# A graph network with sorted neighbours on one core: the gates of the gathers are moved from VectorE to ScalarE

## The chip, the cores and the metric

The kernel runs on one core of a Trainium2 chip. The metric is device time in microseconds (us). Engines are named as in the profile: PE (TensorE), DVE (VectorE), ACT (ScalarE), POOL (GpSimd) and SP (SyncE). Each works through its own list of instructions in order and waits for the others by semaphores. DMAs are issued by SP and, where rows are gathered by index, by POOL.

## The reference

There are 16 graphs of 1024 nodes with 64 channels, and four layers, each a layer norm and a residual around one step on the same adjacency matrix. Cut to what matters:

```python
h = relu(layernorm(x)); x = x + tanh(concat(h, adj @ h) @ W1 + b1) @ W2 + b2        # layer 0
h = relu(layernorm(x)); x = x + (adj + I) @ h / rowsum(adj + I)                     # layer 1
h = relu(layernorm(x)); x = x + mlp(h + quantiles(h of the kept neighbours)) * mask # layer 2
h = relu(layernorm(x)); x = x + (adj @ h) * inv_deg @ W_neighbors + h @ W_self + b  # layer 3
```

Layer 2 is the long one. In a node with more than ten neighbours it removes every k-th neighbour (on both sides of an edge), and then takes for each node and channel the 25%, 50% and 75% quantiles over the neighbours that are left, weighted 0.25, 0.5 and 0.25.

## The kernel before, in words

Each graph passes through six streams, which are Python generators: `adjacency` (load, transpose, find the neighbours to remove, order the nodes by their number of neighbours), `layers` (layers 0 and 1 and the norm of layer 2), `neighbour_lists` (the neighbours' numbers of each node, by repeated top-8 searches on DVE), `gathers`, `sorts` and `tail` (rest of layer 2, layer 3). Several graphs are under way at once.

The nodes are ordered by degree and cut into eight blocks of 128, in five groups k0 to k4 (`GROUPS`). For each group, `gathers` (L1239) fetches the feature rows of the neighbours with one indirect DMA on POOL for each place and block, 128 rows of 256 bytes (L1275): 124 gathers in a graph, 1984 in all, into a single-buffered tile `raw0` to `raw4`. `sorts` runs a pruned sorting network over that tile on DVE (L1308, between `raw` and `other`) and sums the wanted places with their weights (L1327). Places beyond a block's fill are filled by ACT (L1251). POOL also loads key rows for the lists (L1088), packed rows of the few longest nodes (L1256), and gathers the results back to node order (L1347).

The order of all instructions is made when the program is built. A planner (`Clock`, L812) keeps four clocks, `dve`, `pe`, `act` and `pool`. Every stream adds its costs to them by hand and yields the planned time at which it wants to go on; the loop at the end of `direct_path` always resumes the first stream in its list that is due at `clk.dve`, and sets `clk.dve` forward when none is due. `after` (L818) adds the costs of a step to the clocks. A gather adds 1.39 to `clk.pool`, and `gathers` yields `clk.pool - 5` after four of them. So the planner's clocks decide where each instruction stands in its engine's list; the chip decides when it runs.

The gate ties POOL to that plan. Before every four gathers, and before the first key loads of a graph, `gate` (L914) is called. If `clk.dve` is over 3.0 past the last mark, DVE writes a one-element memset (L917), the mark, at its present place in the list, and POOL copies that element (L919), so that it waits until DVE has come as far as the plan had it when these gathers were put in. Eight slots of the mark are used in turn.

Other lines that the text speaks of: preln on DVE and ACT (L848 to L858), where DVE's reduction L853 reads what ACT squared (L851) and L856 what ACT rooted (L854); the neighbour counts that ACT makes in `adjacency` (L956) and DVE adds (L964); signs and keys on ACT (L1024, L1027), positions (L1047, L1050); the eight activations that sum the rows of the transposed adjacency matrix in `layers` (L1212), behind which the planner adds ten units to `clk.act`; the division of layer 1 (L1219).

Of the kernel before, what the change touches and what calls it, by code (L numbers as in the profile page):

```python
# [7 lines left out]
F32 = mybir.dt.float32  # L8
F16 = mybir.dt.float16
BF = mybir.dt.bfloat16  # L10
I32 = mybir.dt.int32
# [6 lines left out]
P = 128  # L18
C = 64
NB = 8  # L20
# [711 lines left out]
def direct_path(ctx: ExitStack, tc: tile.TileContext, t: dict, out: bass.AP, flag):  # L732
# [3 lines left out]
    nc = tc.nc  # L736
# [3 lines left out]
    const = ctx.enter_context(tc.tile_pool(name="const", bufs=1))  # L740
    loads = ctx.enter_context(tc.tile_pool(name="loads", bufs=2))
    graph = ctx.enter_context(tc.tile_pool(name="graph", bufs=1))
    nodes = ctx.enter_context(tc.tile_pool(name="nodes", bufs=2))
# [19 lines left out]
    eps = const.tile([P, 1], F32, name="eps")  # L763
# [51 lines left out]

    clk = Clock()

    def after(dve=0.0, pe=0.0, act=0.0, lat=0.3):  # L818

        clk.dve += dve  # L820
        at = clk.dve
        if pe:
            clk.pe = at = max(clk.pe, at) + pe
        if act:
            clk.act = at = max(clk.act, at) + act
        return at + lat


# [14 lines left out]
    def preln(u, x, ha):  # L843

        s = nodes.tile([P, 4, NB], F32, name="stat")
        xc = mid(u, [P, NB, C])
        sq = mid(u, [P, NB, C])
        nc.vector.tensor_reduce(s[:, 0], x, AX.X, ALU.add)  # L848
        ts(s[:, 1], s[:, 0], 1.0 / C, None, op0=ALU.mult)
        tt(xc, x, s[:, 1, :, None].to_broadcast([P, NB, C]), ALU.subtract)  # L850
        act(sq, xc, AF.Square)  # L851
        yield after(1.5, act=0.65, lat=1.2)
        nc.vector.tensor_reduce(s[:, 2], sq, AX.X, ALU.add)  # L853
        act(s[:, 3], s[:, 2], AF.Sqrt, bias=eps, scale=1.0 / C)  # L854
        yield after(0.7, act=1.0, lat=1.5)
        nc.vector.reciprocal(s[:, 2], s[:, 3])  # L856
        tt(xc, xc, s[:, 2, :, None].to_broadcast([P, NB, C]), ALU.mult)
        act(ha[:, :, :C], xc, AF.Relu)  # L858
        yield after(0.9, act=0.65)
# [45 lines left out]
    def even(v, u):  # L905

        return v.rearrange("c (q u p) -> c u q p", u=2, p=P)[:, u]


    marks = []  # L910
    slots = const.tile([1, 8], F32, name="mark")
    opened = const.tile([1, 2], F32, name="gate")

    def gate():  # L914
        if not marks or clk.dve > marks[-1] + 3.0:
            k = len(marks)
            nc.vector.memset(slots[:, k % 8:k % 8 + 1], 0.0)  # L917
            clk.dve += 0.15
            nc.gpsimd.tensor_copy(opened[:, k % 2:k % 2 + 1], slots[:, k % 8:k % 8 + 1])  # L919
            marks.append(clk.dve)  # L920


    state = [dict() for _ in range(B)]
# [11 lines left out]
    def adjacency(b):  # L935
# [91 lines left out]
            act(p, p, AF.Sign, accum_out=ms[:, i:i + 1])  # L1027
            yield after(0, pe=4.5, act=2.3) - 4.0

        mv = nodes.tile([P, NB], F32, name="mv")  # L1030
        act(mv, ms, AF.Copy, bias=512.0, scale=0.5)
        yield clk.act + 2.0
        key = nodes.tile([P, NB], F32, name="key")
        nc.vector.scalar_tensor_tensor(key, ms, 512.0, cn8, op0=ALU.mult, op1=ALU.add)
        neg = nodes.tile([P, NB], F32, name="neg")
        ts(neg, key, -1.0, None, op0=ALU.mult)
        p = bank2()
        for q in range(2):
# [2 lines left out]
               key[:, 4 * q:4 * q + 4, None].to_broadcast([P, 4, P]), ALU.mult)  # L1041
            nc.tensor.matmul(p[:, q * 512:(q + 1) * 512], onesf, spread.rearrange("p j m -> p (j m)"),
                             start=True, stop=True)
        over = nodes.tile([P, NB], F32, name="over")
        for i in range(NB):
            sink = lists.tile([P, N], F16, tag="ab", name="sink")
            act(sink, p, AF.Sign, bias=neg[:, i:i + 1], accum_out=over[:, i:i + 1])  # L1047
# [1 line left out]
        pos = nodes.tile([P, NB], I32, name="pos", bufs=5)  # L1049
        ts(pos, over, 0.5, 511.5, op0=ALU.mult, op1=ALU.add)  # L1050

        pi = nodes.tile([P, 2, NB], I32, name="pi")
        ts(pi[:, 0], pos, P - 1, None, op0=ALU.bitwise_and)
        ts(pi[:, 1], pos, 7, None, op0=ALU.arith_shift_right)
        ph = nodes.tile([P, 2, NB], F16, name="ph")
        nc.vector.tensor_copy(ph, pi)
        low = lists.tile([P, NB, P], F16, tag="ab", name="low")
        tt(low, pidx[:, None, :].to_broadcast([P, NB, P]), ph[:, 0, :, None].to_broadcast([P, NB, P]), ALU.is_equal)
        high = nodes.tile([P, NB, NB], F16, name="high")
        tt(high, pidx[:, None, :NB].to_broadcast([P, NB, NB]), ph[:, 1, :, None].to_broadcast([P, NB, NB]),  # L1060
           ALU.is_equal)
        both = nodes.tile([P, 2, NB, NB], F16, name="both")
        tt(both[:, 0], high, nid[:, :, None].to_broadcast([P, NB, NB]), ALU.mult)
        tt(both[:, 1], high, mv[:, :, None].to_broadcast([P, NB, NB]), ALU.mult)
        p = bank()
# [3 lines left out]
        m = nodes.tile([P, NB], F32, name="m", bufs=3)  # L1069
# [9 lines left out]
    def neighbour_lists(b):  # L1079
# [5 lines left out]
        def load_keys(i):  # L1085
            if i < NB:
# [4 lines left out]
                ks.append((k, clk.pool + 3.5))  # L1091

        gate()
        for i in range(KB):
            load_keys(i)
# [143 lines left out]
    def gathers(b):  # L1239
        g = state[b]  # L1240
        yield max(g["rows_at"], clk.pool)
        for k, (b0, n, cap, *_) in enumerate(GROUPS):
# [17 lines left out]
            for s in range(cap):  # L1260
                if s % (4 // n) == 0:
                    gate()
                if k == 0 and s == 9:
                    for l, size in enumerate(sizes):
                        nc.sync.dma_start(rows_d[l, :size], packed[:size, l * C:(l + 1) * C])
                if k == 0 and s == 17:
                    for l, p0, s0, ns, nn in PACKS:
                        nc.sync.dma_start(raw[:nn, s0:s0 + ns, :],
                                          rows_d[l, p0:p0 + ns * nn].rearrange("(n s) c -> n s c", s=ns))
                for i in range(n):  # L1270
                    if s >= PLACES[b0 + i]:
                        continue
                    clk.pool += 1.39
                    at = sum(LISTS[:b0 + i]) + s
                    nc.gpsimd.indirect_dma_start(raw[:, s, i * C:(i + 1) * C], None, h_ds[b % 3],  # L1275
                                                 bass.IndirectOffsetOnAxis(ap=g["index"][:, at:at + 1], axis=0))
                if (s + 1) % (4 // n) == 0:
                    yield clk.pool - 5
# [142 lines left out]
    def over_graphs(step, *needs):  # L1421
# [5 lines left out]

    streams = [
        over_graphs(adjacency, ("adjt", 1), ("keys", 1), ("sorts", 3)),
        over_graphs(layers, ("rows", 0), ("tail", 3)),  # L1430
        over_graphs(tail, ("sorts", 0)),
# [23 lines left out]
                assert soonest is not None  # L1455
                clk.dve = soonest

    one = nodes.tile([P, 1], F32, name="one")
    nc.vector.tensor_reduce(one, bad, AX.X, ALU.max)
    p = bank()  # L1460
    nc.tensor.matmul(p[:1, :1], one, onesf[:, :1], start=True, stop=True)
# [3 lines left out]
@with_exitstack  # L1465
def kernel(ctx: ExitStack, tc: tile.TileContext, t: dict, out: bass.AP):
    nc = tc.nc
    pool = ctx.enter_context(tc.tile_pool(name="flag", bufs=1))
    flag = pool.tile([1, 1], I32, name="flag")
    direct_path(tc, t, out, flag)  # L1470
    many = nc.values_load(flag[:1, :1], min_val=0, max_val=P)
    with tc.If(many > 0):
        general_path(tc, t, out)
# [106 lines left out]
```

## Time and profile before

| | |
|---|---|
| median of three runs | 3909.36 us (3884.14 to 3925.28) |
| profiled execution | 3897.33 us, of which the span on the core is 3895.5 us |
| busy DVE / POOL / PE / ACT | 3035.7 / 2644.1 / 2044.1 / 1410.1 us |
| gathers L1275 | 1984, 2148.8 us busy, 1083 ns each in the mean |
| gate copies L919 on POOL | 477, 163.9 us busy, 344 ns each in the mean |
| ACT, one-column-of-eight operations | L1070 (copy from PSUM) 163 ns, L1031 205 ns |
| table loads on ACT | 34 in all, 1283 ns each |

How to read it: busy time is time in which an engine executes, without its waits. A line of a wait list says who waited, for whom, for how many us in total, how often and how long at most. A line of the stretches gives start and end, length, busy time of the five engines with their instruction counts, then the granted clock of PE as a share of full speed, the share of the DMA engines and GB/s. In the chain of waits the profile follows the work back from the last instruction.

### The profile page before, as it was taken

Reading aid. Unit: us, or ns where it says so; the run is one execution under the profiler, and the core shown is the slowest. Engines: PE = TensorE matmul, PEld = TensorE weight load, DVE = VectorE, ACT = ScalarE, POOL = GpSimd, SP = SyncE. Lnnn points to the kernel's source line nnn. Section 1 sums busy time; section 2 is a strip of 40 time slices with the busy share of each in tenths; the row PEclk is TensorE's granted clock in tenths of the full one; section 3 lists DMA queues with packets and bytes.
Section 4 is the critical chain, followed back from the end, with each engine's and each line's share of the span. In section 5 each row is a group of like instructions: output and inputs, shape, how many; then the busy total and the mean of one; then the engine's idle time right before and its main releaser. Section 6 shows DMA issues by size and latency. Waiting matters only on the chain.

```text
span 3895.5 us, 32579 instructions
## 1 busy us (share of the span) xinstructions
PE 2044.1 (52%) x8483; PEld 988.9 (25%) x8483; DVE 3035.7 (78%) x7309; ACT 1410.1 (36%) x2658; POOL 2644.1 (68%) x2792
## 2 busy tenths in 40 slices
PE   6464554646654574646446474565556555741113
PEld 3222222223222232222222232232222323220101
DVE  1557878879687897888787798899699876979482
ACT  5444334243433434333332443443344433430000
POOL 1077576776667686776776777777778686777781
PEclk8666667677676686676666777767677676765555
DMA  2313234152423425242341524243343423232121
GB/s 89 124 39 115 50 99 117 45 172 46 141 68 101 120 65 154 70 125 69 106 106 45 175 51 153 56 142 80 100 119 104 116 55 123 68 105 58 42 52 55
DMA packets 237348, 362.43 MB, mean 93 GB/s; under 512 B 126848, under 2 KB 128496, under 8 KB 237152
## 3 DMA queue, kind: packets, MB, share of 16 engines
q1 hardware_dynamic: 156912, 255.00, 19.0%
q0 software_dynamic: 80096, 104.70, 13.5%
q8 instruction: 69, 1.13, 0.1%
q14 instruction: 127, 1.04, 0.1%
q10 hardware_dynamic: 144, 0.56, 0.0%
HBM read 245.26 MB, written 114.81 MB: 92 GB/s over the span
## 4 chain that ended last, share of the span: by engine, by line
DVE 42%; issue 14%; PE 12%; another core or an unknown queue 9%; ACT 8%; POOL 8%; DMA 5%; SPq 0%; DVEq 0%; ACTq 0%; POOLq 0%
DVE other L1308 12%; DVE raw L1308 11%; POOL raw L1275 6%; PE pt L877 5%; DVE most L1117 4%; ACT adjt L1212 2%; DVE found L1103 2%; DVE agg L1327 2%; ACT sink L1047 2%; DMA k<-keys_d,node 1%; DMA raw<-h_d,index 1%; PE pt L901 1%; DVE k L1112 1%; DVE nb L942 1%
## 5 line engine op out<-in xcount | busy, mean ns | idle before, releaser
L1275 POOL DMA_INDIRECT raw<-h_d,index x1984 | 2148.8, 1083 | 559.0 <-issue 533.1
L1308 DVE TENSOR_TENSOR other<-raw 128x512 f32<-128x512 f32 (+11 forms) x816 | 536.7, 688 | 151.7 <-DMA raw<-h_d,index 113.9
L877 PE MATMUL pt<-adjt,ha 128*65 128x512 f32 (+1 forms) x1024 | 485.4, 635 | 44.6 <-DVE ha L1199 30.6
L919 POOL COPY gate<-mark 1x1 f32<-1x1 f32 x477 | 163.9, 344 | 416.2 <-DVE mark L917 369.3
L949 PE MATMUL pt<-ef,a 128*128 128x128 f32 x1024 | 207.5, 360 | 320.8 <-ACT adjt L950 129.6
L1308 DVE TENSOR_TENSOR raw<-other 128x512 f32<-128x512 f32 (+10 forms) x464 | 355.9, 792 | 5.8 <-DVE other L1308 0.6
L991 PE MATMUL pt<-eh,nbt 128*128 128x512 f16 (+3 forms) x1024 | 213.8, 365 | 266.5 <-ACT nbt L980 192.2
L1117 DVE MAX8 most<-k 128x8 uint16<-128x1024 uint16 x208 | 255.4, 1228 | 13.2 <-DVE k L1112 3.3
L949 PEld LDWEIGHTS pt<-ef,a 128*128 128x128 f32 x1024 | 157.7, 185 | 408.2 <-issue 180.6
L1024 ACT ACTIVATE nb<-pt 128x1024 f16<-128x1024 f32 x128 | 130.6, 1020 | 317.1 <-remote 118.4
L877 PEld LDWEIGHTS pt<-adjt,ha 128*65 128x65 f32 (+1 forms) x1024 | 148.1, 148 | 364.1 <-issue 360.1
L950 ACT COPY adjt<-pt 128x512 f32<-128x512 f32 x256 | 139.1, 583 | 250.0 <-remote 146.4
L956 ACT ACTIVATE nb<-nb 128x512 f16<-128x512 f16 x256 | 159.6, 629 | 179.3 <-DVE nb L942 70.2
L1308 DVE TENSOR_TENSOR raw<-other,raw 128x640 f32<-128x640 f32 (+3 forms) x448 | 216.5, 494 | 4.9
L1308 DVE TENSOR_TENSOR raw<-raw,other 128x128 f32<-128x128 f32 (+7 forms) x496 | 211.5, 436 | 6.1
L1020 PE MATMUL pt<-eh,gone 128*128 128x128 f16 x1024 | 129.7, 257 | 162.7 <-DVE gone L1000 76.5
L878 ACT COPY big<-pt 64x1024 f32<-64x1024 f32 (+1 forms) x32 | 32.2, 1007 | 496.1 <-PE pt L877 300.6
L1308 DVE TENSOR_TENSOR other<-other,raw 128x128 f32<-128x128 f32 (+4 forms) x448 | 201.4, 460 | 4.2
L1384 PE MATMUL tm<-at,ha 128*64 128x512 f32 x512 | 174.1, 785 | 50.0 <-DMA at<-adjt_d 44.4
L1103 DVE MAX8 found<-k 128x8 f32<-128x1024 f16 x128 | 156.3, 1221 | 51.2 <-DMA k<-keys_d,node 51.2
L991 PEld LDWEIGHTS <-nbt 128*128 128x128 f16 x1024 | 105.0, 116 | 359.4 <-ACT nbt L980 203.2
L1347 POOL DMA_INDIRECT res<-agg_d,pos x128 | 135.7, 1060 | 74.9 <-DMA agg_d<-agg 37.4
(182 smaller groups left out, 4350.6 us busy)
## 6 DMA issues: line engine op xcount, KB each, us to landing
a<-in_adj_dram SPq DMA_DIRECT2D x64, 1024.0 KB
adjt_d<-adjt SPq DMA_DIRECT2D x64, 1024.0 KB
at<-adjt_d SPq DMA_DIRECT2D x128, 512.0 KB
keys_d<-nb SPq DMA_DIRECT2D x64, 512.0 KB
raw<-h_d,index POOLq DMA_INDIRECT x1984
x<-in_x_dram SPq DMA_DIRECT2D x16, 256.0 KB
h_d<-h SPq DMA_DIRECT2D x16, 256.0 KB
agg_d<-agg SPq DMA_DIRECT2D x16, 256.0 KB
```

The costliest lines, as they stand in the source:

```text
L877: nc.tensor.matmul(p[p0:p0 + n, s], h[:, j, :n], adjt[:, j, s], start=j == 0, stop=j == NB - 1)
L919: nc.gpsimd.tensor_copy(opened[:, k % 2:k % 2 + 1], slots[:, k % 8:k % 8 + 1])
L949: nc.tensor.transpose(p[:, u * P:(u + 1) * P], a[:, j * P:(j + 1) * P], identf)
L950: nc.scalar.copy(adjt[:, 4 * q:4 * q + 4, i * P:(i + 1) * P], p.rearrange("p (u m) -> p u m", m=P))
L956: act(nb[:, i, s], nb[:, i, s], AF.Copy, accum_out=mn[:, q, i:i + 1])
L991: nc.tensor.matmul(p[:, o:e], nbt[:, j, :], stair[:, :e - o], start=j % 4 == 0, stop=j % 4 == 3)
L1103: nc.vector.max(out=found[:, o:o + 8], in_=src)
L1117: nc.vector.max(out=most, in_=less.bitcast(U16))
L1275: nc.gpsimd.indirect_dma_start(raw[:, s, i * C:(i + 1) * C], None, h_ds[b % 3], bass.IndirectOffsetOnAxis(ap=g["index"][:, at:at + 1], axi ...
L1308: tt(view(two[to], *((i, vi) if greater else (j, vj)), w), view(two[s], i, vi, w), view(two[u], j, vj, w), ALU.max if greater else ALU.min)
L1347: nc.gpsimd.indirect_dma_start(res[:, i, :], None, g["agg_d"], bass.IndirectOffsetOnAxis(ap=g["pos"][:, i:i + 1], axis=0))
L1384: nc.tensor.matmul(p[q * C:(q + 1) * C, :], ha[:, j, :], even(ats[j], q), start=j == 0, stop=j == NB - 1)
```

## The change

`gate` no longer makes a mark. A new function `mark`, called in `after` whenever a step has a cost on ACT, makes ACT copy one element into a slot behind the work just planned, if `clk.act` is over 3.0 past the last mark; it adds 0.2 to `clk.act`. Some steps that the planner charges to ACT by hand make no mark. `gate` looks through the last 20 marks for the latest whose planned time lies more than 1.0 before `clk.pool`, and lets POOL copy it; if there is none, or it is the one that was waited for last, it does nothing. There are 32 slots. In the built programs the 477 memsets on DVE and 477 copies on POOL become 513 copies on ACT and 363 copies on POOL. As marks no longer add 0.15 to `clk.dve` but 0.2 to `clk.act`, other instructions change their places too. The tiles `mv`, `key`, `neg`, `over`, `pi`, `ph`, `high`, `both` and `one` have one buffer in place of two.

```diff
+    marks, gates = [], []
+    slots = const.tile([1, 32], F32, name="mark")
+    opened = const.tile([1, 2], F32, name="gate")
+
+    def mark():
+        if not marks or clk.act > marks[-1][0] + 3.0:
+            t = slots[:, len(marks) % 32:len(marks) % 32 + 1]
+            nc.scalar.copy(t, eps[:1])
+            clk.act += 0.2
+            marks.append((clk.act, t))
+
+    def gate():
+
+        due = [m for m in marks[-20:] if m[0] < clk.pool - 1.0]
+        if due and gates[-1:] != due[-1:]:
+            gates.append(due[-1])
+            nc.gpsimd.tensor_copy(opened[:, len(gates) % 2:len(gates) % 2 + 1], due[-1][1])
+
     def after(dve=0.0, pe=0.0, act=0.0, lat=0.3):
...
         if act:
             clk.act = at = max(clk.act, at) + act
+            mark()
         return at + lat
...
-    marks = []
-    slots = const.tile([1, 8], F32, name="mark")
-    opened = const.tile([1, 2], F32, name="gate")
-
-    def gate():
-        if not marks or clk.dve > marks[-1] + 3.0:
-            k = len(marks)
-            nc.vector.memset(slots[:, k % 8:k % 8 + 1], 0.0)
-            clk.dve += 0.15
-            nc.gpsimd.tensor_copy(opened[:, k % 2:k % 2 + 1], slots[:, k % 8:k % 8 + 1])
-            marks.append(clk.dve)
...
-        mv = nodes.tile([P, NB], F32, name="mv")
+        mv = nodes.tile([P, NB], F32, name="mv", bufs=1)
...
-        pi = nodes.tile([P, 2, NB], I32, name="pi")
+        pi = nodes.tile([P, 2, NB], I32, name="pi", bufs=1)
```

More of the change, by code (lines that the diff above doesn't have):

```diff
@@ L1028, in adjacency @@
             yield after(0, pe=4.5, act=2.3) - 4.0
-        mv = nodes.tile([P, NB], F32, name="mv")
+        mv = nodes.tile([P, NB], F32, name="mv", bufs=1)
         act(mv, ms, AF.Copy, bias=512.0, scale=0.5)
         yield clk.act + 2.0
-        key = nodes.tile([P, NB], F32, name="key")
+        key = nodes.tile([P, NB], F32, name="key", bufs=1)
         nc.vector.scalar_tensor_tensor(key, ms, 512.0, cn8, op0=ALU.mult, op1=ALU.add)
-        neg = nodes.tile([P, NB], F32, name="neg")
+        neg = nodes.tile([P, NB], F32, name="neg", bufs=1)
         ts(neg, key, -1.0, None, op0=ALU.mult)
@@ L1043, in adjacency @@
                              start=True, stop=True)
-        over = nodes.tile([P, NB], F32, name="over")
+        over = nodes.tile([P, NB], F32, name="over", bufs=1)
         for i in range(NB):
@@ L1050, in adjacency @@
         ts(pos, over, 0.5, 511.5, op0=ALU.mult, op1=ALU.add)
-        pi = nodes.tile([P, 2, NB], I32, name="pi")
+        pi = nodes.tile([P, 2, NB], I32, name="pi", bufs=1)
         ts(pi[:, 0], pos, P - 1, None, op0=ALU.bitwise_and)
         ts(pi[:, 1], pos, 7, None, op0=ALU.arith_shift_right)
-        ph = nodes.tile([P, 2, NB], F16, name="ph")
+        ph = nodes.tile([P, 2, NB], F16, name="ph", bufs=1)
         nc.vector.tensor_copy(ph, pi)
@@ L1058, in adjacency @@
         tt(low, pidx[:, None, :].to_broadcast([P, NB, P]), ph[:, 0, :, None].to_broadcast([P, NB, P]), ALU.is_equal)
-        high = nodes.tile([P, NB, NB], F16, name="high")
+        high = nodes.tile([P, NB, NB], F16, name="high", bufs=1)
         tt(high, pidx[:, None, :NB].to_broadcast([P, NB, NB]), ph[:, 1, :, None].to_broadcast([P, NB, NB]),
            ALU.is_equal)
-        both = nodes.tile([P, 2, NB, NB], F16, name="both")
+        both = nodes.tile([P, 2, NB, NB], F16, name="both", bufs=1)
         tt(both[:, 0], high, nid[:, :, None].to_broadcast([P, NB, NB]), ALU.mult)
@@ L1456, in direct_path @@
                 clk.dve = soonest
-    one = nodes.tile([P, 1], F32, name="one")
+    one = nodes.tile([P, 1], F32, name="one", bufs=1)
     nc.vector.tensor_reduce(one, bad, AX.X, ALU.max)
```

## The prediction

> **What bounds the kernel now.** I read the page from the top: busy shares, the 40 slices, the chain that ended last, then the waits of each engine, then busy time by stretches of about one graph.
>
> ```profile
> span 3895.5 us, 32579 instructions
> PE 2044.1 (52%) x8483; PEld 988.9 (25%) x8483; DVE 3035.7 (78%) x7309; ACT 1410.1 (36%) x2658; POOL 2644.1 (68%) x2792
> ...
> DVE 42%; issue 14%; PE 12%; another core or an unknown queue 9%; ACT 8%; POOL 8%; DMA 5%; SPq 0%; DVEq 0%; ACTq 0%; POOLq 0%
> ```
>
> The reader is to see that VectorE (DVE) is the fullest engine and holds 42% of the chain, while POOL, which issues the gathers, holds 8% and ScalarE (ACT) 8%. No engine is a bound alone: 58% of the chain is elsewhere. The stretches say where DVE is the limit (columns: stretch, length, then PE, PEld, DVE, ACT, POOL busy):
>
> ```profile
> 1130.00:1358.00 228.00, 127.56 (x538) 61.33 (x538) 190.26 (x459) 89.62 (x169) 165.71 (x174) 0.71 0.35 99
> 2938.00:3161.00 223.00, 127.48 (x579) 62.55 (x578) 200.84 (x484) 97.26 (x180) 168.99 (x174) 0.70 0.38 106
> 3391.00:3612.00 221.00, 76.89 (x241) 33.26 (x240) 189.05 (x459) 40.39 (x76) 168.30 (x174) 0.64 0.29 77
> 3612.00:3810.00 198.00, 30.86 (x98) 15.80 (x98) 123.69 (x312) 5.84 (x13) 149.95 (x163) 0.54 0.20 47
> ```
>
> In the middle a graph takes about 228 us and DVE works 190 to 200 of them (83 to 90%). In the last two stretches the adjacency work has run out, DVE has 32 and 74 us to spare, and POOL's gathers follow each other without a break. So: DVE and its waits set the middle, POOL the last graph. What DVE waits for in the middle (435 to 3391 us):
>
> ```profile
> DVE stat L853 <- ACT mid L851: 86.2, 10, 16.8
> DVE stat L856 <- ACT stat L854: 54.6, 5, 19.0
> DVE mn L964 <- ACT nb L956: 46.3, 5, 13.6
> DVE found L1103 <- DMA k<-keys_d,node: 42.3, 8, 14.4
> DVE other L1308 <- DMA raw<-h_d,index: 31.3, 9, 8.7
> ```
>
> ACT is its first reason by far. The gathers cost it 31.3 us, with the patched rows (8.9) and their packing (8.5 over the whole run) about 49. The gates themselves:
>
> ```profile
> L917 DVE MEMSET mark<- x477: 59/59/59, 142.8 to 3796.2; 1x1 f32 x159
> L919 POOL COPY gate<-mark x477: 177/237/1471, 143.0 to 3804.8; 1x1 f32<-1x1 f32 x159
> ...
>   DVE mark L917: 369.3, 65
> ```
>
> POOL stands at 65 of 477 gates for 369.3 us, 124.5 of which is the first gate of all, where the keys are not there anyway. That leaves 245 us, 15 a graph.
>
> [...] the 128x8 activation L1031 takes 205 ns, the 128x8 copy from PSUM (L1070) 163. I take 0.20 us for a mark. [...] a gather takes 0.94 us at its shortest and 1.083 in the mean. [...]
>
> **The change part by part.** I compared the instruction lists of both kernels. Apart from marks and gates the same instructions stand on every engine.
>
> 1. DVE loses 477 memsets: 477 x 59 ns = 28.1 us of busy time. DVE is 83 to 90% busy in the middle, but part of the time gained is spent in the same waits for ACT. I count 0.6 of it: -17 us (ends: 0, all hidden by waits; -28, all on the path).
>
> 2. ACT gains 513 one-element copies: 513 x 0.20 = 103 us, busy 1410 to 1513. What hides it is ACT's idle 64%. It is not hidden where ACT is late for DVE. The chain has ACT at 8% of the span, 312 us; of that the L1212 and L1047 blocks (2% each) have no mark inside. On the remaining 156 us marks add 103/1410 = 7%: +11 us, and I take +12 (ends: 0; +50, if each of DVE's 52 waits for ACT, 334 us in the whole run, grows by five marks).
> Each mark may have to wait until the gate that last read its slot is through; with 32 slots that is 32 marks back, some 240 us at 3895/513 = 7.6 us a mark, so no wait.
>
> 3. POOL loses 114 gates (477 to 363). A gate between two gathers takes 0.18 + 0.16 us where the gathers alone have a gap of 0.30, so 0.04 us at its shortest, 0.20 at its mean of 0.344. 114 x 0.04 to 0.20 = 5 to 23 us of POOL, which in the middle only turns into waiting at the next gate. In the last two graphs, 2/16 of it, POOL is the path: -3 us.
>
> 4. The wait changes its source: 245 us for DVE marks go, waits for ACT marks come. Behind a gate stand the next four or more gathers, key loads (L1088) and the result gathers (L1347); behind those the sort that reads `raw`. To size it I took, for each of the 363 gates, the ACT instruction in front of its mark and the gather behind the gate, and compared their times in the trace of before. In 313 cases ACT was through before the gather started (median 16 us). In 50 it was later; these sum to 491 us. In the first six graphs, where the two orders still run alike, it is 12 or so holds of 4 to 31 us, about 25 us a graph, against 15 for DVE now. Against that, gates no longer hold POOL when DVE alone stalls: at 1245 to 1253 us POOL stood 7.16 us for a mark that DVE reached only after a 15.09 us stall at L1219, while ACT had been idle since 1240. More in some places, less in others: I take 0 (ends: -60, if DVE's 49 us for gathers vanish and the end gains a little; +110, worked out under the slower rival).
>
> 5. The planner's order moves. Its clock charged DVE 0.15 for each gate and now charges ACT 0.2 for each mark. Two in three DVE instructions stand at another place, 18 places away in the mean. The drift has a direction: in the planner's own clock the keys of graph 15 come 63 later, its rows 40 later, the last sort at the same point. Of a planned 198 per graph that is about a quarter of a graph's adjacency and list work. L1308 and L1327 hold 1905 of DVE's 3035.7 us, so other work is 1131/16 = 71 us a graph; a quarter, 18 us, moves from the full middle to the last stretches with 32 and 74 us to spare. I count two thirds: -12 us (ends: -40, +40, for what a shuffle of in-order queues can do either way).
>
> 6. Single buffers for `mv`, `key`, `neg`, `over`, `pi`, `ph`, `high`, `both`: each is written once a graph and read within tens of us, so the next write, some 228 us later, finds it free: 0. If they were needed closer together, it would cost one short wait per graph.
>
> Sum: -17 + 12 - 3 + 0 - 12 = -20 us, so 3895.5 becomes 3875 in span. The profiled execution took 3897.3 us; the median of the three runs shown is 3909.4, 12 above it, and they spread from 3884 to 3925. On the median's footing: 3909 - 20 = 3889, I say 3890. About 1% (39 us) is what a measurement of this kernel can tell from no change.
>
> **The rivals.**
> *Looser gates (faster).* POOL stops sharing DVE's stalls, runs some us ahead, and every sort finds its rows. Then DVE's 49 us for gathers go, the marks count in full (28), and the end gains 20 of the 72 us that DVE waits for DMA after 3391: -97, 3812. For it: ACT is 16 us ahead in the median of those 313. Against it: the late sixth of the gates, and that gathers are not DVE's main wait.
> *ACT marks stand late (slower).* One mechanism: the mark behind the eight L1212 activations is dated before the ten units that the planner adds for that block, but it runs after it (8.4 us, 1232.0 to 1240.4). 15 gates are tied to such marks, in the third gather group, where in the trace of before seven ACT ends were 3 to 17 us late. The sort of that group starts within 10 us of its last gather in nine of 16 graphs. A hold decides once it exceeds that margin, some 4 us net: with 10 us held, 6 reach DVE in every graph, 16 x 6 = +96, up to +110 with the marks of L1027 and L956: 4005. Against it: DVE often comes late to that same sort, since it waits for the same ACT and PE work.
> *Nothing but a shuffle.* Gates matter little at all, and only the new order of the DVE queue speaks: within 40 us of before, either sign.
>
> **How the numbers follow.** Forecast with its small gain, and the shuffle inside 1%: 0.38, own range 3870 to 3945. Looser gates 0.25 and a lucky shuffle 0.04: faster 0.29. Late ACT marks 0.25 and an unlucky shuffle or ACT queue 0.08: slower 0.33. The range reaches into both: 3800 holds nearly all of the faster case, 3990 about two thirds of the slower one.
>
> **What would show it.** Step 1: no DVE memsets of `mark`, DVE busy near 3008. Step 2: 513 ACT copies of 0.2 us, ACT near 1513; the waits of L853, L856 and L964 for ACT stay near 187 us. Step 4: gate waits of POOL on ACT between 200 and 400 us; DVE's waits for `raw` near 49 in the middle. Step 5: PE and ACT busier after 3391. Gate waits far below 200 with fewer waits for `raw` would mean the faster rival; DVE waits for `raw` of 120 or more, with POOL standing behind L1212 marks, the slower one. The forecast is wrong if waits for ACT grow by more than 50 us.

## The result and the profile after

Before took 3898.16 us (3875.60 to 3934.30) and after 3902.82 us (3866.82 to 3932.16), medians of 20 runs each. The ratio is 1.0003 with an interval of [0.9978, 1.0028]: no change that this measurement can tell. Runs over 1.5% above the fastest of their kernel (three of after) are left out of the ratios. The profiled execution of after took 3922.63 us, 20 above its own median, while that of before lay 1 below its median here; so 25 us of difference between the two pages are mostly this choice of executions.

From the page of after: busy shares and the chain.

```profile
PE 2056.5 (52%) x8483; PEld 995.1 (25%) x8483; DVE 3044.8 (78%) x6832; ACT 1447.9 (37%) x3171; POOL 2610.6 (67%) x2678
...
DVE 34%; issue 13%; PE 13%; POOL 12%; ACT 11%; another core or an unknown queue 10%; DMA 6%; SPq 0%; DVEq 0%; ACTq 0%; POOLq 0%
```

DVE has 477 instructions fewer (7309 to 6832) and is as busy as before. Its 59 ns memsets had overlapped with their neighbours: without them the trace of before has 3035.5 us of busy DVE time, with them 3035.7. ACT grew by 37.8 us for 513 marks, 74 ns each.

The stretches of after (columns as in the prediction):

```profile
1130.00:1358.00 228.00, 132.31 (x525) 63.13 (x525) 186.89 (x420) 88.17 (x194) 160.32 (x165) 0.67 0.35 99
...
3391.00:3612.00 221.00, 103.84 (x388) 45.24 (x388) 174.11 (x384) 61.88 (x125) 158.56 (x156) 0.67 0.29 82
3612.00:3810.00 198.00, 32.72 (x98) 17.01 (x98) 141.56 (x328) 8.66 (x25) 134.27 (x128) 0.53 0.21 47
```

After 3391 PE and ACT have more to do (103.84 and 61.88 us against 76.89 and 40.39). But this trace ends 25 us later, so the last 505 us of each trace are the fairer comparison. Here they are for before, for after, and for a kernel of the experiments below, which has ACT gates and the old order:

```profile
3390.50:3895.50 505.00, 138.17 (x438) 64.66 (x437) 335.14 (x820) 51.89 (x98) 326.29 (x345) 0.59 0.24 62
...
3415.80:3920.80 505.00, 158.67 (x536) 73.08 (x534) 329.53 (x744) 64.17 (x140) 301.56 (x297) 0.59 0.24 64
...
3359.40:3864.40 505.00, 153.64 (x501) 70.42 (x499) 351.58 (x798) 63.16 (x144) 320.84 (x315) 0.59 0.24 65
```

PE and ACT do have more work there (PE 20 us, ACT 12 us), but most of that is also there with the old order, and DVE, whose work the prediction expected to move, has none more than before. DVE's waits in the middle, 435 to 3391 us:

```profile
DVE den L1226 <- remote: 95.3, 8, 13.7
DVE stat L873 <- ACT mid L871: 58.9, 7, 12.5
DVE other L1315 <- DMA raw<-h_d,index: 50.4, 19, 10.7
DVE pos L1057 <- ACT mark L826: 46.8, 9, 8.4
```

The waits of the layer norms for ACT are smaller (the lines that were L853, L856 and L964 have 58.9, 4.1 and 13.5 us, against 187). That for the gathers is 50.4 us, against 31.3 and 8.9 for the patched rows; over the whole span the two sums are 121.2 and 122.8. Two new ones lead: `den` L1226, "remote", which is to say that the wait ended although nothing in the trace ended just then, and `pos` L1057 behind the sign passes on ACT. The gate, by its tiles:

```profile
L826 ACT COPY mark<-eps x513: 173/173/192, 19.4 to 3908.3; 1x1 f32<-1x1 f32 x171
L835 POOL COPY gate<-mark x363: 177/215/2180, 201.5 to 3770.5; 1x1 f32<-1x1 f32 x182
...
  ACT mark L826: 332.4, 46
```

POOL stands at 46 gates for 332.4 us. Ten of the holds, 12.5 us each in the mean, are behind the sign passes of L1054 (125.1 us), four behind the block of L1219 (46.5 us), ten behind the counts of L963 (55.5 us) and 14 behind L1002 (56.4 us).

### The profile page after: what moved, and what is told of

The parts are those of the page before. It is cut to its first block, busy times and chain, and to the rows that moved or that the text cites. A ratio compares the mean times of both kernels' runs of the same rounds, so it can differ in the third digit from the quotient of the medians.

```text
span 3920.8 us, 32419 instructions
## 1 busy us (share of the span) xinstructions
PE 2056.5 (52%) x8483; PEld 995.1 (25%) x8483; DVE 3044.8 (78%) x6832; ACT 1447.9 (37%) x3171; POOL 2610.6 (67%) x2678
## 3 DMA queue, kind: packets, MB, share of 16 engines
q0 software_dynamic: 80096, 104.70, 13.5%
## 4 chain that ended last, share of the span: by engine, by line
DVE 34%; issue 13%; PE 13%; POOL 12%; ACT 11%; another core or an unknown queue 10%; DMA 6%; SPq 0%; DVEq 0%; ACTq 0%; POOLq 0%
POOL raw L1282 10%; DVE other L1315 8%; DVE raw L1315 7%; PE pt L897 5%; DVE most L1124 5%; ACT adjt L1219 3%; DVE found L1110 3%; ACT sink L1054 2%; DMA raw<-h_d,index 2%; DVE agg L1334 2%; PE pt L921 1%; POOL res L1354 1%; DMA k<-keys_d,node 1%; DVE k L1119 1%
## 5 line engine op out<-in xcount | busy, mean ns | idle before, releaser
L1315 DVE TENSOR_TENSOR other<-raw 128x512 f32<-128x512 f32 (+11 forms) x816 | 534.7, 688 | 138.6 <-DMA raw<-h_d,index 121.2
L897 PE MATMUL pt<-adjt,ha 128*65 128x512 f32 (+1 forms) x1024 | 495.8, 646 | 100.8 <-DVE ha L1206 97.9
L998 PE MATMUL pt<-eh,nbt 128*128 128x512 f16 (+3 forms) x1024 | 231.7, 389 | 327.8 <-ACT nbt L987 243.6
L835 POOL COPY gate<-mark 1x1 f32<-1x1 f32 x363 | 116.2, 320 | 349.5 <-ACT mark L826 332.4
L956 PE MATMUL pt<-ef,a 128*128 128x128 f32 x1024 | 200.2, 348 | 168.8 <-issue 58.4
L1095 POOL DMA_INDIRECT k<-keys_d,node x128 | 129.1, 1008 | 182.5 <-DVE node L1080 125.1
L1391 PE MATMUL tm<-at,ha 128*64 128x512 f32 x512 | 184.0, 815 | 118.2 <-DMA at<-adjt_d 90.2
L963 ACT ACTIVATE nb<-nb 128x512 f16<-128x512 f16 x256 | 158.8, 622 | 203.1 <-DVE nb L949 74.5
L1031 ACT ACTIVATE nb<-pt 128x1024 f16<-128x1024 f32 x128 | 130.2, 1017 | 262.5 <-PE pt L1030 104.2
L956 PEld LDWEIGHTS pt<-ef,a 128*128 128x128 f32 x1024 | 151.4, 179 | 267.6 <-issue 155.4
```

The source lines that it names most:

```text
L897: nc.tensor.matmul(p[p0:p0 + n, s], h[:, j, :n], adjt[:, j, s], start=j == 0, stop=j == NB - 1)
L956: nc.tensor.transpose(p[:, u * P:(u + 1) * P], a[:, j * P:(j + 1) * P], identf)
L963: act(nb[:, i, s], nb[:, i, s], AF.Copy, accum_out=mn[:, q, i:i + 1])
L998: nc.tensor.matmul(p[:, o:e], nbt[:, j, :], stair[:, :e - o], start=j % 4 == 0, stop=j % 4 == 3)
L1031: act(nb[:, i, :], p, AF.Relu)
L1095: nc.gpsimd.indirect_dma_start(k, None, g["keys_d"], bass.IndirectOffsetOnAxis(ap=g["node"][:, i:i + 1], axis=0))
```

## The experiments

The first eight kernels ran on one chip, in two groups of four, beside which before took 3895 and 3842 us; the last four on another, where before took 3664 us. The chip of the first measurement is not on record; the 3898 us of before there are near those beside the first four, and below it is counted with the first chip. Ratios are always to the runs of before taken beside the kernel.

**No gates at all.** My theory after the result was that gates only park POOL in time that it has to spare. The two kernels keep the order of after and of before, and the planner's charges, and drop marks and gates.

```diff
-            nc.scalar.copy(t, eps[:1])                                # e1; e2: the memset
-            nc.gpsimd.tensor_copy(opened[...], due[-1][1])            # e1; e2: its copy
```

> The changed kernel with neither marks nor gates; the planner's charges stay, so every other instruction keeps its place. My theory (gates only park POOL in time that it has to spare): POOL's 332 us of gate waits move to other waits or go, DVE's waits for gathers change by less than 40 us, time within 0.7% of before (3870 to 3925). Rival A (gates hold the gathers back on a path that matters): 60 us or more faster, below 3840. Rival B (gates protect something[...]): 60 us or more slower.

> The kernel before with neither marks nor gates, the planner's charge of 0.15 kept, so every other instruction keeps its place. My theory: within 0.7% of before, at most 20 us faster for the memsets that DVE no longer has. Rival A: 60 us or more faster. Rival B: 60 us or more slower. If this and the other kernel without gates lie apart by over 20 us, the order is worth more than the gates.

Measured: 4648.7 us, ratio 1.1935 [1.1889, 1.1981], and 4674.0 us, 1.2004 [1.1952, 1.2055]. The theory fell: without gates the kernel takes about 750 us longer in the one order, 780 in the other. From the page of the first:

```profile
PE 2092.3 (45%) x8483; PEld 1018.0 (22%) x8483; DVE 3056.2 (65%) x6832; ACT 1406.3 (30%) x2658; POOL 2376.0 (51%) x2315
...
DVE 35%; another core or an unknown queue 25%; PE 10%; issue 10%; ACT 10%; POOL 7%; DMA 3%; SPq 0%; DVEq 0%; ACTq 0%; POOLq 0%
```

No engine works more than 3% longer; 25% of the chain, against 10% in after, is waits that nothing in the trace ended. In sixteen stretches of 83 to 146 us POOL's gathers follow each other without a break. They are 34% of the span and hold 60% of DVE's waits of this kind ("remote" or "issue", 364 of 611 us) and 58% of ACT's. In the twelve of 83 to 86 us, taken together, DVE is 0.98 busy in the first ten us, 0.93 in the fourth ten and 0.23 in the seventh; ACT goes from 0.77 to 0.01. These twelve recur at about the same place of each graph's work, so part of that fall can belong to the place. Here is how it looks, in the timeline of that kernel:

```profile
1461.76 0.29 DVE L1313 TENSOR_TENSOR raw<-raw,other 128x128 f32<-128x128 f32 x1 [1.45 <-DVE raw L1313]
...
1490.36 0.95 POOL L1280 DMA_INDIRECT raw<-h_d,index  x1 [0.30 <-issue]
...
1497.58 1.01 ACT L896 COPY big<-pt 65x1024 f32<-65x1024 f32 x1 [64.39 <-remote]
```

The sort's instruction of 0.29 us waits 1.45 us for the one ahead of it on its own engine, and ACT, whose PE input stood ready by 1463, begins 6 us after the last gather of the run has ended.

**Source and order apart.** Two kernels complete a square: the order of after with gates tied to DVE, and that of before with gates tied to ACT. Apart from marks and gates, each has the instructions of the kernel whose order it has, in the same order. The kernels of the new order have 363 gates each; in the old order they are 477 on DVE and 382 on ACT, so in that row the number of gates changes with the source, and so do the buffers.

```diff
+            t = slots[:, len(gates) % 8:len(gates) % 8 + 1]           # e3, from after
+            nc.vector.memset(t, 0.0)
+            nc.gpsimd.tensor_copy(opened[...], t)
...
-            clk.act += 0.2                                            # e4, from after: marks without a charge
...
+        if not charged or clk.dve > charged[-1] + 3.0:                # on clk.act, and the old charge on clk.dve
+            clk.dve += 0.15
+            charged.append(clk.dve)
```

> The changed kernel's order of instructions and its 363 gates, but each gate waits for a memset that DVE does at that place, as before; no marks on ACT. My theory (the source of the wait does not matter): between 3880 and 3920, as both kernels. Rival (ACT marks cost and the new order gains, or the other way about, and they cancel): 25 us or more away from the changed kernel's 3903, faster if the ACT marks cost.

> The order of the kernel before, with marks on ACT (526 of them) and gates that wait for them (382) by the rule of the changed kernel; the planner charges as before, so nothing else changes its place; the single buffers are there too. My theory: 3880 to 3925. Rival (the source of the wait costs, the order gains, and they cancel): 25 us or more above the kernel before.

| | gates tied to DVE | gates tied to ACT |
|---|---|---|
| order of before | 1 | 0.9899 [0.9874, 0.9923] |
| order of after | 1.0100 [1.0062, 1.0138] | 1.0003 [0.9978, 1.0028] (the change, from its own measurement) |

The new source gains 1.0% in both rows, 39 us; the new order costs 1.0% in both columns, 39 us. On this chip, and within the intervals shown, the change is the sum of two effects that cancel, and the top right kernel, 3860.2 us, beats the three others.

One place where the two orders differ in these four traces is the division. The kernel with the order of before and ACT gates has, of all DVE's waits there,

```profile
DVE den L1228 <- PE pt L1215: 27.9, 2, 25.9
DVE den L1228 <- PE pt L1051: 3.9, 2, 3.2
```

32 us over the whole span. With the order of after it is 163 us under ACT gates (120.1 of them "remote") and 200 under DVE gates (126.8 "remote"); before has 64:

```profile
DVE den L1219 <- remote: 40.7, 5, 15.1
...
DVE den L1226 <- remote: 120.1, 10, 13.7
```

Total waits of DVE differ by less, 773 us in after against 754, because its waits for ACT in the layer norms and counts shrank: 207 us over the whole span before and 146 with ACT gates in the old order; in the new order 47 with DVE gates and 96 with ACT gates. What happens at the division comes back in ten graphs of after; the timeline of one:

```profile
1661.89 1.93 PE L1049 MATMUL pt<-spread,ef 128*128 128x512 f32 x4
...
1668.09 0.18 POOL L835 COPY gate<-mark 1x1 f32<-1x1 f32 x1
1668.52 0.69 DVE L873 TENSOR_REDUCE stat<-mid 128x8 f32<-128x512 f32 x1 [6.44 <-ACT adjt L1219]
1668.75 0.96 POOL L1282 DMA_INDIRECT raw<-h_d,index  x1 [0.48 <-issue]
...
1677.51 0.94 POOL L1282 DMA_INDIRECT raw<-h_d,index  x1 [0.30 <-issue]
1681.83 0.21 DVE L1226 RECIPROCAL den<-pt 128x8 f32<-128x8 f32 x1 [12.62 <-remote]
1681.92 1.11 ACT L1054 ACTIVATE sink<-pt,neg 128x1024 f16<-128x1024 f32 x1 [13.43 <-remote]
```

DVE and ACT both want products that PE, by its records, finished by 1663.82. Eight gathers run from 1668.75 to 1678.45, then POOL stands at a gate, and 3.4 us later both engines start within 0.1 us of each other. Over the whole of after, 15 waits of DVE above 4 us end on nothing visible; in 10 of them POOL had just been idle for over 1 us, where a random moment in the middle has a chance of 0.09. For ACT it is 39% of 75, for PE none of 20. So such a wait often ends in a pause of POOL, not always; that the pause ends it is not shown, for here POOL's own gate waited for ACT.

PE has no record from 1663.82 up to the two starts, at 1681.83 and 1681.92, so this trace doesn't show whether its last product came late or only the signal of it. On the other chip, below, the same place shows no such wait.

Nor is the wait at the division a fixed price of the order. The kernel with four ACT copies for each mark (below) has every other instruction where after has it and ran on the same chip, and waits there for 63 us, as before does:

```profile
DVE den L1227 <- remote: 11.8, 6, 3.7
```

So the 39 us of the order are measured on this chip; through which waits they come is not shown.

**Copies without a tie.** Does a break in the gathers suffice? One constant copy stands on POOL in place of each gate.

```diff
-            nc.gpsimd.tensor_copy(opened[...], due[-1][1])
+            nc.gpsimd.tensor_copy(opened[...], eps[:1])
```

> The changed kernel's order and its 363 copies on POOL, but each copies a constant, so that no gate waits for another engine; no marks. Theory S (an unbroken stream of gathers starves the other engines, and any ordinary POOL operation in between breaks it): the starving is gone, 3850 to 3950. Theory W (POOL must be held back, the copy itself does nothing): as without gates, above 4500.

> The order of the kernel before with its 477 copies on POOL, each of a constant, so that no gate waits; no marks. Theory S: 3850 to 3950. Theory W: above 4500.

Measured: 4350.7 us, 1.1328 [1.1293, 1.1362], and 4282.8 us, 1.1159 [1.1119, 1.1198]. A copy among the gathers takes back a third to two fifths of the loss. Whether the rest needs POOL to be held at the right moments, or only longer pauses, these two don't tell.

**What a mark costs.** Four memsets for each mark in before, and four copies for each in after.

```diff
-            nc.vector.memset(slots[...], 0.0)        # e8: nc.scalar.copy(t, eps[:1])
+            for _ in range(4):
+                nc.vector.memset(slots[...], 0.0)
```

> The kernel before with four memsets in place of one at each mark; nothing else moves. In the trace of before the start of the next DVE instruction is 41 ns later behind a memset, so DVE gets 3 x 477 x 41 ns = 59 us more work. If DVE's marks lie on the path as I counted (0.6): +35 us. If DVE has time to spare: under +10. If the removal of the memsets is the whole gain of the ACT gates (39 us for 20 us of DVE work): +110.

> The changed kernel with four copies on ACT in place of one at each mark; nothing else moves. A mark delays the next ACT instruction by 73 ns, so ACT gets 3 x 513 x 73 ns = 112 us more work. Prediction's step 2 (11 us for 103 us of ACT): +12 us. If ACT lies on the path with most of it: +60 or more.

Measured: 1.0052 [1.0030, 1.0074], so 1431 more memsets cost 20 us, and by their number the 477 that the change removes about 7. That is rather too much: the added ones show in DVE's busy time (3116.6 us, 57 ns each), the single ones hardly do. After with four copies: 1.0067 [1.0043, 1.0090] against 1.0003 for after itself, measured beside other runs of before, so 0.6% (0.2 to 1.1) or 25 us for 1539 more copies. By their number that makes 8 us for the 513. But the copies of one mark, which all write one slot, start 222 ns apart in the median and add 188 ns each to ACT's busy time (1736.8 us), where a single mark adds 74 and the instruction behind it starts 82 ns after it. By busy time it is 3 us, an estimate. And since the wait at the division is gone in this kernel, the 25 us may not be the copies alone.

**Paced copies, late marks, charges** (the other chip).

```diff
+            for u in range(5):                                            # e9: no marks
+                nc.gpsimd.tensor_copy(opened[:, u % 2:u % 2 + 1], eps[:1])
...
-        due = [m for m in marks[-20:] if m[0] < clk.pool - 1.0]           # e10
+        due = [m for m in marks[-20:] if m[0] < clk.pool - 1.0 and not m[2]]   # m[2]: made at L1054 or L1219
...
+        if not charged or clk.dve > charged[-1] + 3.0:                    # e11: both charges
+            clk.dve += 0.15
+            charged.append(clk.dve)
...
-            clk.act += 0.2                                                # e12: neither
```

> The order of the changed kernel; at each of its 363 gates GpSimd makes five copies of a constant and waits for no other engine; ScalarE's marks are left out. One such copy per gate gave 1.133 of the kernel before, none gave 1.194, the gate tied to a mark 1.000. Theory 'pace' (all that matters is that the gathers come thinner; five copies of about 0.18 us and their gaps are about as much GpSimd time as the 332 us for which the changed kernel's gates wait): under 1.02. Theory 'tie' (GpSimd has to be held at the moments when the other engines are behind): over 1.07, since the copies are spread over all moments alike.

> The changed kernel, but no gate is tied to a mark behind the ten Sign passes of L1054 or the block of L1219, whose marks held GpSimd some 12 us each time; the gate takes the mark before these (333 gates in place of 363, same order elsewhere). Theory 'late marks cost' (the rival of the prediction, in small): GpSimd's waits at gates fall by about 150 us and the time by 20 to 40 us, ratio 0.990 to 0.995. Theory 'these holds are hidden or even of use': the waits fall, the time stays within 0.3% or rises, ratio 0.998 to 1.02.

> Gates tied to ScalarE as in the changed kernel; the planner is charged 0.15 us on VectorE's clock at the places where the kernel before made a memset and 0.2 us on ScalarE's at each mark, which gives an order of its own (370 gates, 502 marks). With ScalarE marks the order planned with VectorE's charge alone gave 0.990 and that with ScalarE's alone 1.000. Theory 'ScalarE's charge spoils the order': 1.000 or more. Theory 'the missing VectorE charge spoils it': 0.990. Theory 'orders scatter by about a per cent whatever their reason': anything from 0.985 to 1.015, and the fourth order (no charge) doesn't fit with either of the others.

> Gates tied to ScalarE as in the changed kernel, and the planner is charged for neither memsets nor marks (369 gates, 525 marks, an order of its own). Theory 'ScalarE's charge spoils the order': 0.990. Theory 'the missing VectorE charge spoils it': 1.000 or more. Theory 'orders scatter by about a per cent whatever their reason': anything from 0.985 to 1.015.

*Paced copies*: 3894.6 us, 1.0628 [1.0612, 1.0644], between both theories. As this chip shows next to no waits without a visible end (8 us on DVE and none on ACT or PE in this trace), it can't tell what longer pauses would do on the first one. Against the kernel without late marks, of the same order on the same chip (3651.5 us), it loses 243 us, and DVE's waits for what POOL brings explain it. With paced copies:

```profile
DVE other L1315 <- DMA raw<-h_d,index: 289.3, 45, 24.7
DVE found L1110 <- DMA k<-keys_d,node: 89.8, 18, 8.3
```

and without late marks:

```profile
DVE other L1323 <- DMA raw<-h_d,index: 101.1, 22, 21.1
DVE found L1115 <- DMA k<-keys_d,node: 34.0, 13, 3.6
```

That is 244 us more. Constant copies also slow POOL when it is the late one: it has 60% of the chain here, and 26% without late marks. A tied gate holds it only when it is ahead of the mark; in the kernel without late marks that is at 29 of 333 gates.

*Late marks*: 0.9961 [0.9947, 0.9974], POOL's waits at gates 81.0 us. The ratio lies between the two forecasts, and after itself was not measured on this chip, so what the late marks cost stays open.

*Charges*: both give 1.0117 [1.0102, 1.0133], neither 1.0190 [1.0176, 1.0204]. With ACT gates, DVE's charge alone gave 0.990 and ACT's alone 1.000 on the first chip. If ACT's charge spoilt the order, the kernel with neither would be fast; if the missing charge of DVE did, the one with both would. Neither holds: the orders scatter by a per cent or two, whatever makes them differ. (Across chips this is no strict comparison; these two alone differ by 0.7%.) In neither is it the division, where DVE waits for 30 and 26 us.

The other chip showed more than I asked. In the four traces taken there PE has no wait at all that nothing visible ends ("remote", or "issue", where the profile shows no event within 1 us before the start), ACT one of 0.2 us, and DVE 5 to 15 us of them. On the first chip ACT alone has 905 us in after, and 1021 in the kernel with the order of before and ACT gates, though that is the faster one: the sum of such waits is not a cost in itself. The clock granted to PE doesn't tell the two chips apart: it was 0.693 in the trace with both charges on the second chip, and 0.696 in that with four ACT copies on the first, where ACT has 846 us. The place shown above looks like this in the kernel without late marks:

```profile
1580.82 1.93 PE L1051 MATMUL pt<-spread,ef 128*128 128x512 f32 x4
...
1586.40 0.94 POOL L1290 DMA_INDIRECT raw<-h_d,index  x1 [0.30 <-issue]
...
1587.33 1.09 ACT L1056 ACTIVATE sink<-pt,neg 128x1024 f16<-128x1024 f32 x1
1587.65 0.94 POOL L1290 DMA_INDIRECT raw<-h_d,index  x1 [0.30 <-issue]
1588.06 0.20 DVE L1234 RECIPROCAL den<-pt 128x8 f32<-128x8 f32 x1
```

Apart from two gates, which this kernel doesn't have here because they were tied to late marks, these are the same instructions in the same order, with gathers as dense as there, and both engines go on at once; `den` waits 28.4 us in the whole span, 163 in after. So the order of the program alone does not explain why DVE and ACT stand in after. What it is, and why one chip has it, isn't in these traces: the order without gates was not run on the second chip, and whether gates are worth anything there stays open.

## Why the prediction was right, and where not

The number was right, 3890 against 3903, and so was the forecast that the difference would be too small to tell. It was right by luck, because two effects cancelled: one step had the wrong sign, another was mis-sized the other way.

1. *Memsets, -17*: -7 at most, by the fourfold memsets. The step took 0.6 of 28.1 us; DVE's busy time did not fall to 3008 but stayed at 3044.8, since nearly all of the 59 ns lay inside the time of other instructions.
2. *ACT copies, +12*: about +3 to +8, an estimate. Their length was nearly right (173 ns, estimated at 0.20 us), but a single one adds only 74 ns to ACT's busy time, so ACT came to 1447.9 and not 1513. The 0.20 us, between the 163 and 205 ns of L1070 and L1031, is near what a copy adds behind another one into the same slot (188 ns), and not what a single mark costs. The waits of the layer norms and counts for ACT did not stay near 187 us in the middle but fell to 76; over the whole span they fell most with the new order.
3. *Fewer gates, -3*, and 6. *single buffers, 0*: not tried alone. They are inside the -39 us of the kernel with the order of before and ACT gates.
4. *Source of the wait, 0*: that kernel gains 39 us [30, 49] by steps 1 to 4 and 6, and 1 and 2 come to about nothing. In the new order, where gates and buffers are the same in number, ACT gates gain 38. So this step is near -40, inside its own ends of -60 to +110. POOL's waits were sized well (279.5 us in the middle, forecast 200 to 400). What failed is what they were thought to do. The step looked for late gathers, and DVE's wait for `raw` hardly moved (40.2 to 50.4 us in the middle with the patched rows, 122.8 to 121.2 in all). The prediction's 49 us held 8.5 us of packing over the whole run besides. Without gates the kernel takes 750 us longer though no engine has over 3% more to do, and most of the waits without a visible end fall into runs of gathers (60% of DVE's, 58% of ACT's). That was in no term of the sum. Through which waits the new source gains its 39 us is not shown.
5. *Order, -12*: +39 us. This is the step that failed. It expected some 18 us of DVE's work to move from the full middle into the last stretches; in the last 505 us DVE is busy for 329.5 us, against 335.1 before, so none did. Outside the sorts, where the adjacency work is, it is 69.7 against 70.7. What costs the 39 us stays open: in the trace of after `den` stands some 12 us in ten of the 16 graphs while gathers run, but the kernel of the same order with four copies a mark stood there no longer than before. The ends of 40 either way did hold it, for what a shuffle can do.

Of the rivals, *ACT marks stand late* named marks that do hold POOL (those of L1212, L1027 and L956 are behind 17 of the 46 holds, 112 us), but not the ones with most of it, behind the sign passes (ten holds, 125 us). Some 14 to 20 us after each of the four holds of the L1212 block a sort waits 2 to 10 us for its rows. From graph 6 on the holds don't reach the sorts: that of the third group waits about 1 us, because DVE itself is late from the same block, as the rival's "against" had it. *Looser gates* failed, since waits for gathers stayed. *Nothing but a shuffle* had the size of the order's effect, and was wrong that gates matter little: without them the kernel takes 19% longer.

## What to carry to other kernels

When a change moves a wait and also feeds a planner, build the square of old and new order with old and new wait before crediting either; here each is worth 1% on one chip and they cancel. A wait that seems only to idle an engine can be what the other engines live on (without the gates this kernel takes 19 to 20% longer), so take it out once, alone, and see. And look at how much of the chain ends on nothing visible: that share is no engine's work, a sum of durations doesn't hold it, and it differed here between chips (on one of them none on PE and 0.2 us on ACT) and between times on one chip (3 and 7% of the chain with four memsets and four copies, 9 and 10% in before and after). And a wait at one line, though two kernels of one order show it, need not be the price of that order: here a third with the same order lacks it.

## What was not expected of the hardware

On one chip, with unbroken indirect gathers on POOL (0.94 us each at the shortest and 0.30 between), DVE fell from 0.98 to 0.23 busy and ACT from 0.77 to 0.01 within some 70 us, with durations of instructions unchanged (1220 ns for the 128x1024 step of the sort, 1223 in after). A third or so of ACT's waits of over 4 us without a visible end (39% of 75 in after) ended in a pause of POOL, a median 2.9 us into it in after and 5.7 us in the kernel without gates. On another chip the same kernel was 5 to 6% faster (3664 us for before, against 3842 and 3895), and the traces of four other kernels there showed no such wait on PE, and none above 0.2 us on ACT. What held up DVE and ACT beside such gathers, no run here shows.
